# Asking for the routed tiles' rows and weights at the end of attention, turning their rows one output earlier, and collecting the last list one tile later

## The chip, the core and the metric

The kernel runs on one core of a Trainium2 chip. The metric is device microseconds of one execution, lower is better; the time quoted for a kernel is the median of its runs. A profile is one further execution, with a record of every instruction on each engine: TensorE (PE, with its weight loads as PEld), VectorE (DVE), ScalarE (ACT), GpSimd (POOL) and SyncE (SP).

## What is computed

Two layers act on `x` (4 batches, 512 tokens, 256 features, float32). Each has a gated cross-attention with 16 heads and a gated feed-forward part. The last feed-forward part is a routed one: each token goes to the one of four experts with the largest logit. Cut to what matters here:

```python
x = x + tanh(g_xattn[0]) * L0_xattn(layernorm(x), ctx)      # biases, time decay, output projection
x = x + tanh(g_ffn[0])   * L0_ffn(layernorm(x))             # ternary weights, relu
x = x + tanh(g_xattn[1]) * L1_xattn(layernorm(x), ctx)      # relu on q, k, v
# L1_ffn on h = layernorm(x), tokens t, experts e:
expert_idx = argmax(h @ W_router, -1)
a = gelu(einsum('th,ehi->tei', h, W1) + b1)                 # only the chosen expert's row is kept
y = a[t, expert_idx[t]] @ Wo + bo + h
x = x + tanh(g_ffn[1]) * (layernorm(y) * gamma + beta)
```

## The kernel before

**Attention.** The attention of both layers is a loop over 128 units `u`, four to a group of four heads; there are 32 groups. `scores(u, vs)` issues the score products (line 494): four for the maxima of a later unit (`pm`, drained on DVE by line 508) and four for the weights of this unit (`psc`, drained on ACT by the exponential in line 523). The maxima run six units ahead, so units 122 to 127 have weights alone. `slot(u)` then fills the unit with other work. Every fourth unit it does `weighted` (line 551, the product with the values) and two units later `shifted` and `divided` (lines 565, 602). What else goes in is chosen by a planner: chains of steps, each with a cost in TensorE microseconds, a `gap` (how many units must lie between it and the step before it) and a due unit. A step is taken when its chain is ready and the unit's cost stays about under `SLOT = 3.1`, or when it is due. A step that costs 0 is taken at once.

**The routed part.** The 2048 tokens are sorted by expert into 19 tiles of 128. `route(b)` normalises batch `b` (`stats`, `more_stats`, `norm`), stores the rows to the scratch `rows_d`, turns them, computes logits (`products`, line 738, `logits`, line 748) and ranks (line 764). `dispatch(i)` builds three lists of tiles: list 0 from two batches gives tiles 0 to 4, list 1 from three batches gives tiles 5 to 8, and list 2, complete, gives tiles 9 to 18. Its steps are small VectorE operations (`lists`, `token_places`, `by_tile`, `picked` in line 899, `by_expert`), then two steps that need TensorE: `collected` (line 912) and `tokens` (line 921), which end in the row numbers `get`. For a tile `j`, `fetch_rows(j)` (line 950) and `fetch_weights(j)` (line 962) are indirect DMAs issued by POOL, of 262 KB and 1.05 MB. `turn_tile(j)` (line 974) transposes the tile's rows on PE and copies them to `xs`. `hidden_half(j, f2)` (line 996) does half of the hidden products, 16 products per half, and the Gelu (line 1009). `output_tile(j)` (line 1178) does the 16 output products, `norm_tile` the layer norm on DVE with one POOL power (line 1193), and `put_tile` stores a tile by an indirect DMA on POOL (line 1205).

**What sets the order.** Within an engine instructions run in the order written; PE, DVE, ACT and POOL are scheduled by hand. Tiles 0 to 3 have their hidden products within attention (chain `ahead`, ready at `u0 + 3` of the second-layer batch 2), with the Gelu left for later. Then comes the part behind attention: the last hidden half of tile 3, the last `weighted`, `turn_tile(4)`, the last `divided`, a change of buffer pools from `att` to `moe`, the routing of the last batch (`stats3`, `more3`, `norm3`, with its layer norm on DVE and the reciprocal root on POOL, lines 330 to 340), and a queue of hidden (`"h"`) and output (`"o"`) items. In the kernel before, an `"h"` item ends with the transpose of the next tile. `steps` hangs the routing's and the last list's pieces behind items of that queue. A buffer ring limits the fetches: five row buffers (`xr`) and, for weights, two plus three.

The order of the queue before is: h4 (with the turn of 5), o0, o1, turn3, o2, products3, o3, logits3, h5 (with the turn of 6), ranks3 and the first list steps, o4, the picks, h6 (with the turn of 7), collected, o5, tokens, fetch 9, h7 (with the turn of 8), o6, h8, o7, then tile 9 and so on.

Of the kernel before, what the change touches and what calls it, by code (L numbers as in the profile page):

```python
# [20 lines left out]
B, S, D = 4, 512, 256  # L21
# [14 lines left out]
T_ALL = TT + NE - 1  # L36
# [12 lines left out]
def flamingo_kernel(ctx: ExitStack, tc: tile.TileContext, t: dict, out: bass.AP):  # L49
    nc = tc.nc  # L50
# [654 lines left out]
    def route(b, eng=None):  # L705

        st = {}

        def stats():
            st["xn"] = act.tile([P, NT, D], F32, tag="xn", name=f"xn_f1_{b}")  # L710
            first, st["more"], st["rows"] = layernorm(
                x[b], st["xn"], 1e-5, f"f1_{b}", eng
            )
            first()

        def more_stats():
            st["more"]()

        def norm():
            st["rows"]()  # L720
            (eng or nc.gpsimd).tensor_tensor(
                x[b], x[b], bet1.unsqueeze(1).to_broadcast([P, NT, D]), ALU.add
            )
            rd = rows_d[b * S : (b + 1) * S, :].rearrange("(n p) d -> p n d", p=P)
            nc.sync.dma_start(out=rd[:, :, 0:D], in_=st["xn"])
            nc.sync.dma_start(out=rd[:, :, D : 2 * D], in_=x[b])

        def turn():
            st["xT"] = act.tile([P, NC, S], F32, tag="blocks", name=f"xTf1_{b}", bufs=1)
            transposed(st["xn"], st["xT"], f"f1_{b}")  # L730

        def products():


            plT = bank_psum(f"plT{b}")[:, 0:P]
            for c in range(NC):
                for n in range(NT):
                    nc.tensor.matmul(
                        plT[n * HP : (n + 1) * HP, :], lhsT=wr[:, c, :], rhs=st["xT"][:, c, ts(n, P)],
                        start=(c == 0), stop=(c == NC - 1),  # L740
                    )
            st["lT"] = const.tile([P, P], F32, tag="dec", name=f"lT{b}")
            nc.scalar.copy(st["lT"], plT)

        def logits():

            plg = bank_psum(f"plg{b}")[:, 0:P]
            nc.tensor.transpose(plg, st["lT"], ident)
            plg = plg.rearrange("p (n e) -> p n e", e=HP)[:, :, 0:NE]
            top = sml.tile([P, NT], F32, tag="top", name=f"top{b}")  # L750
            nc.vector.tensor_reduce(top, plg, AX.X, ALU.max)
            oh = onehot[:, ts(b, NT), :]
            nc.vector.tensor_tensor(oh, plg, top.unsqueeze(2).to_broadcast([P, NT, NE]), ALU.is_ge)
            nc.vector.tensor_tensor(oh, oh, order, ALU.mult)
            nc.vector.tensor_reduce(top, oh, AX.X, ALU.max)
            nc.vector.tensor_tensor(oh, oh, top.unsqueeze(2).to_broadcast([P, NT, NE]), ALU.is_equal)

        def ranks():
            prk = bank_psum(f"prk{b}")[:, 0 : 2 * NT * NE].rearrange(
                "p (i n e) -> p i n e", i=2, e=NE  # L760
            )
            oh = onehot[:, ts(b, NT), :]
            for i, m in enumerate((before, ones)):
                nc.tensor.matmul(prk[:, i], lhsT=m, rhs=oh, start=True, stop=True)
            for n in range(NT):
                k = b * NT + n
                nc.vector.tensor_tensor(count[:, k + 1, :], count[:, k, :], prk[:, 1, n, :], ALU.add)
            nc.vector.tensor_tensor(
                rank[:, ts(b, NT), :], prk[:, 0], count[:, b * NT : (b + 1) * NT, :], ALU.add
            )  # L770

        return [
            (stats, 0, 0), (more_stats, 0, 1), (norm, 0, 1), (turn, 0.9, 1), (products, 0.6, 1),
            (logits, 0.2, 1), (ranks, 0.5, 1),
        ]
# [167 lines left out]
    def fetch_rows(j):  # L943

        have = max(n for n, first in LISTS if first <= j or n == LISTS[0][0]) * S
        if j in (3, *range(LISTS[1][1], T_ALL)) and made["behind"]:
            xg[j] = act.tile([P, 2 * D], F32, tag="xr", name=f"xr{j}", bufs=5)
        else:
            xg[j] = wts.tile([P, 2 * D], F32, tag="xg", name=f"xg{j}", bufs=4)
        nc.gpsimd.indirect_dma_start(  # L950
            out=xg[j], out_offset=None, in_=rows_d[0:have, :],
            in_offset=bass.IndirectOffsetOnAxis(ap=get[:, j : j + 1], axis=0),
            bounds_check=have - 1, oob_is_err=False,
        )

    def fetch_weights(j):

        if j < T_AHEAD or (j - T_AHEAD) % 5 < 2:
            wg[j] = weight_place(f"wg{j}")
        else:  # L960
            wg[j] = act.tile([P, NC * FF + NF], F32, tag="wg", name=f"wg{j}", bufs=3)
        nc.gpsimd.indirect_dma_start(
            out=wg[j], out_offset=None, in_=t["w1e"],
            in_offset=bass.IndirectOffsetOnAxis(ap=wrow[:, j : j + 1], axis=0),
            bounds_check=NE * P - 1, oob_is_err=False,
        )
# [51 lines left out]
    n_units = len(groups) * NT  # L1018
# [15 lines left out]
    for b in range(B):  # L1034
        first, rest = ffn0(b)
# [26 lines left out]
    def step(f, *args, cost=0, gap=0):  # L1062
        return (lambda: f(*args), cost, gap)

    def tile_steps(j):
        return [
            step(turn_tile, j, cost=0.3), step(hidden_half, j, 0, cost=1.75, gap=int(j == 0)),
            step(hidden_half, j, 1, cost=1.75),
        ]

    for b in range(B - 1):
        u0 = first_unit(1, b + 1)
        if b == 0:
            chain(route(b), u0 + 4, u0 + 13)
        elif b == 1:
            turn_0, *rest_0 = tile_steps(0)
            ahead = chain(
                [
                    *route(b), *dispatch(0), step(fetch_rows, 0), step(fetch_weights, 0),
                    step(fetch_rows, 1), step(fetch_weights, 1), step(fetch_rows, 2),  # L1080
                    step(fetch_rows, 3), (turn_0[0], turn_0[1], 2), *rest_0, step(fetch_rows, 4),
                    step(fetch_weights, 2, gap=1), *tile_steps(1), step(fetch_rows, 0),
                    step(fetch_weights, 3, gap=1), *tile_steps(2), step(fetch_rows, 1),
                    step(fetch_weights, 4, gap=1), *tile_steps(3)[:2],
                ],
                u0 + 3, n_units - 1,
            )
        else:
            routed = chain(route(b), u0 + 2, u0 + 9)
            chain(dispatch(1), n_units - LEAD, n_units - 1, routed)  # L1090
# [124 lines left out]
    for f2 in range(2):  # L1215
# [4 lines left out]
    att.__exit__(None, None, None)  # L1220
    act = ctx.enter_context(tc.tile_pool(name="moe", bufs=2))
    made["behind"] = True
    stats3, more3, norm3, turn3, products3, logits3, ranks3 = (job for job, *_ in route(B - 1, nc.vector))
    lists, token_places, by_tile, *sels, by_expert, collected, tokens = (job for job, *_ in dispatch(2))
    stats3()
    more3()
    norm3()


    steps = {  # L1230
        ("o", 1): [turn3], ("o", 2): [products3], ("o", 3): [logits3],
        ("h", 5): [ranks3, lists, token_places, by_tile], ("o", 4): [*sels, by_expert],
        ("h", 6): [collected], ("o", 5): [tokens],
    }
    first = LISTS[-1][1]
    queue = [("h", 4), *(("o", j) for j in range(4)), ("h", 5)]
    for j in range(4, T_ALL - 2):
        queue += [("o", j), ("h", j + 2)]
    queue.remove(("o", first - 1))
    queue.insert(queue.index(("h", first)), ("o", first - 1))  # L1240
    queue += [("o", T_ALL - 2), ("o", T_ALL - 1)]
    for j in (5, 3, 6, 7):
        fetch_rows(j)
        if j > 3:
            fetch_weights(j)
    for kind, j in queue:
        if kind == "h":
            for f2 in range(2):
                hidden_half(j, f2)
            if j + 1 < T_ALL and j + 1 != first:  # L1250
                turn_tile(j + 1)
        else:
            if j + 1 == first:
                turn_tile(first)
            if j < 3:
                for f2 in range(2):
                    activated(j + 1, f2)
            output_tile(j)
            norm_tile(j)
            if j > 0:  # L1260
                put_tile(j - 1)
        for job in steps.pop((kind, j), ()):
            job()
        fetch = {("o", 4): [8], ("o", 5): [9], ("o", 6): [10], ("o", 7): [11], ("o", 8): [12]}.get((kind, j))
        if fetch is None and kind == "o" and first <= j < T_ALL - 4:
            fetch = [j + 4]
        for i in fetch or ():
            fetch_rows(i)
            fetch_weights(i)
    put_tile(T_ALL - 1)  # L1270
    assert not steps

# [74 lines left out]
```

## Time and profile before

| what | value |
|---|---|
| median of 3 runs | 870.73 us (870.62 to 871.59) |
| the profiled execution's own time | 872.11 us |
| its span, first to last instruction | 870.4 us |
| mean granted TensorE clock | 0.987 of full |
| PE busy | 825.7 us (95%) |
| DVE, ACT, POOL busy | 563.8, 422.4, 278.9 us |
| bytes moved by DMA | 43.07 MB |

The page's first part gives busy time by engine, its second part cuts the span in 40 slices of 21.8 us (a digit 9 is 90% or more busy). The timeline lists instructions in order of time, equal neighbours merged, with the idle time before them in square brackets and what ended it. The table by windows gives busy time per engine in chosen stretches, the clock that was granted, and the DMA engines' share and rate. All times are from the start of the span. Attention ends and the routed tiles begin at about 716 us; the last 142 us of PE work are the tiles.

### The profile page before, as it was taken

Reading aid. Unit: us, or ns where it says so; the run is one execution under the profiler, and the core shown is the slowest. Engines: PE = TensorE matmul, PEld = TensorE weight load, DVE = VectorE, ACT = ScalarE, POOL = GpSimd, SP = SyncE. Lnnn points to the kernel's source line nnn. Section 1 sums busy time; section 2 is a strip of 40 time slices with the busy share of each in tenths; the row PEclk is TensorE's granted clock in tenths of the full one; section 3 lists DMA queues with packets and bytes.
Section 4 is the critical chain, followed back from the end, with each engine's and each line's share of the span. In section 5 each row is a group of like instructions: output and inputs, shape, how many; then the busy total and the mean of one; then the engine's idle time right before and its main releaser. Section 6 shows DMA issues by size and latency. Waiting matters only on the chain. (4 is left out here: it accounts for less than half of the span.)

```text
span 870.4 us, 13598 instructions
## 1 busy us (share of the span) xinstructions
PE 825.7 (95%) x5241; PEld 464.3 (53%) x5241; DVE 563.8 (65%) x1218; ACT 422.4 (49%) x886; POOL 278.9 (32%) x446
## 2 busy tenths in 40 slices
PE   6999999999999999999999999989999996899994
PEld 3444454435463347445555445644445545798993
DVE  6778778766856784778546864586875544843443
ACT  2475565554545452646355563366545564223331
POOL 5536365424332432401110210021033215344542
PEclk9999999999999999999999999999999998999998
DMA  9100000000000000000000010001043216055540
GB/s 319 52 1 1 1 2 2 1 1 0 2 13 25 1 1 1 26 1 1 1 1 25 1 49 1 1 1 50 1 146 110 74 62 242 26 194 173 199 162 14
DMA packets 18096, 43.07 MB, mean 49 GB/s; under 512 B 2222, under 2 KB 12208, under 8 KB 15600
## 3 DMA queue, kind: packets, MB, share of 16 engines
q0 software_dynamic: 5488, 28.13, 9.3%
q1 hardware_dynamic: 12128, 13.54, 4.6%
q8 instruction: 41, 0.67, 0.3%
q10 hardware_dynamic: 416, 0.54, 0.2%
q14 instruction: 23, 0.19, 0.1%
HBM read 35.91 MB, written 6.68 MB: 49 GB/s over the span
## 5 line engine op out<-in xcount | busy, mean ns | idle before, releaser
L508 DVE TENSOR_REDUCE m<-pm 128x1 f32<-128x512 f32 x512 | 317.1, 682 | 115.6 <-PE psc L494 112.1
L523 ACT ACTIVATE p<-psc 128x512 f32<-128x512 f32 x512 | 266.8, 603 | 154.5 <-PE psc L494 152.3
L494 PE MATMUL psc<-q,k 32*128 32x512 f32 x1024 | 280.4, 624 | 0.2 <-DVE h L672 0.2
L494 PE MATMUL pm<-k,q 32*128 32x512 f32 x1024 | 263.1, 617 | 1.3 <-ACT q L481 0.9
L526 POOL TENSOR_TENSOR p<-p,dec 128x256 f32<-128x256 f32 x128 | 93.6, 735 | 178.8 <-ACT p L523 178.8
L494 PEld LDWEIGHTS pm<-k,q 32*128 32x128 f32 x1024 | 93.1, 185 | 84.1 <-issue 50.1
L494 PEld LDWEIGHTS psc<-q,k 32*128 32x128 f32 x1024 | 106.9, 184 | 53.8 <-issue 27.3
L551 PE MATMUL po<-p,v 128*32 128x512 f32 x1024 | 116.5, 595 | 2.9 <-DVE m L508 2.9
L996 PE MATMUL pg<-xs,wg 128*128 128x128 f32 x608 | 74.1, 280 | 4.8 <-ACT xs L977 4.1
L996 PEld LDWEIGHTS pg<-xs,wg 128*128 128x128 f32 x608 | 72.1, 195 | 8.2 <-ACT xs L977 4.8
L551 PEld LDWEIGHTS po<-p,v 128*32 128x32 f32 x1024 | 31.7, 109 | 82.9 <-issue 60.5
L619 POOL TENSOR_TENSOR x<-x,o 128x256 f32<-128x256 f32 x14 | 10.2, 728 | 189.7 <-DVE o L612 128.3
L1178 PE MATMUL pyf<-wo,ha 128*128 128x256 f32 x304 | 70.6, 388 | 0.0
L1009 ACT ACTIVATE ha<-pg,wg 128x128 f32<-128x128 f32 x120 | 34.2, 368 | 71.3 <-PE pg L996 69.4
L1178 PEld LDWEIGHTS pyf<-wo,ha 128*128 128x128 f32 x304 | 57.9, 195 | 7.9 <-issue 0.4
L664 PE MATMUL ph<-xTf,w1q 128*128 128x512 f32 x128 | 60.0, 605 | 0.0
L379 PE MATMUL py_f<-w2q,h 128*128 128x256 f32 x256 | 57.2, 381 | 0.0
L557 ACT COPY oT<-po 128x512 f32<-128x512 f32 x32 | 18.7, 585 | 78.7 <-PE po L551 78.7
L379 PEld LDWEIGHTS py_f<-w2q,h 128*128 128x128 f32 x256 | 48.0, 190 | 9.4 <-DVE m L508 3.0
L1182 DVE TENSOR_TENSOR y<-y,pyf 128x256 f32<-128x256 f32 x19 | 8.0, 421 | 55.5 <-PE pyf L1178 54.9
L451 PE MATMUL pk<-cT,wk 128*128 128x512 f32 x68 | 35.4, 645 | 7.6 <-DMA cT<-in_ctxT_dram 7.3
L664 PEld LDWEIGHTS ph<-xTf,w1q 128*128 128x128 f32 x128 | 22.6, 189 | 30.4 <-issue 18.2
(223 smaller groups left out, 814.2 us busy)
## 6 DMA issues: line engine op xcount, KB each, us to landing
x<-in_x_dram SPq DMA_DIRECT2D x4, 512.0 KB, 6.7
rows_d<-xn_f SPq DMA_DIRECT2D x4, 512.0 KB, 3.0
rows_d<-x SPq DMA_DIRECT2D x4, 512.0 KB, 3.0
cT<-in_ctxT_dram SPq DMA_DIRECT2D x3, 512.0 KB, 9.1
w1q<-in_w_dram SPq DMA_DIRECT2D x1, 1024.0 KB
w2q<-in_w_dram SPq DMA_DIRECT2D x1, 1024.0 KB, 11.1
wo<-in_wo_dram SPq DMA_DIRECT2D x2, 512.0 KB
rows<-in_rows_dram SPq DMA_DIRECT2D x1, 640.0 KB, 9.0
```

Of the source, the lines that this page charges most:

```text
L379: nc.tensor.matmul(py[:, n, :], lhsT=operand(c, n0 + n), rhs=w[:, c, :], start=(c == 0), stop=(c == chunks - 1),)
L451: nc.tensor.matmul(pp, lhsT=attn_w[layer][w][:, c, ts(tt, P)], rhs=src[:, c, :], start=(c == 0), stop=(c == NC - 1),)
L494: nc.tensor.matmul(out_, lhsT=lhs[r, ts(n, P)], rhs=rhs[r, :], start=True, stop=True)
L508: nc.vector.tensor_reduce(m[:, n, 2 * pair + i, r : r + 1], pm[i], AX.X, ALU.max)
L523: nc.scalar.activation(p[:, i, :], psc[i], AF.Exp, scale=SCALE)
L526: nc.gpsimd.tensor_tensor(d, d, dec.unsqueeze(1).to_broadcast([P, 2, P]), ALU.mult)
L551: nc.tensor.matmul(po[i * HP : (i + 1) * HP, :], lhsT=v_sb[b % 2][0][:, kt, c0 : c0 + HP], rhs=ps_exp[NT * s + kt, i // 2][:, i % 2, :], s ...
L557: nc.scalar.copy(pos[s], po)
L664: nc.tensor.matmul(ph, lhsT=w1q[:, c, ts(f, P)], rhs=st["xT"][:, c, :], start=(c == 0), stop=(c == NC - 1),)
L996: nc.tensor.matmul(ph[:, f, :], lhsT=w[:, c, ts(f2 * NF // 2 + f, P)], rhs=xs[j][:, c, :], start=(c == 0), stop=(c == NC - 1),)
L1009: nc.scalar.activation(ha[:, f, :], (ha if src is None else src)[:, f, :], AF.Gelu, bias=biases[j][:, fa : fa + 1],)
L1178: nc.tensor.matmul(py, lhsT=hs[j, f // 4][:, f % 4, :], rhs=wo1[f // 4][:, f % 4, :], start=(f == 0), stop=(f == NF - 1),)
```

## The change

Four things change.

1. In the planner, each `tile_steps` has a gap of one unit between a tile's transpose and its first hidden half (before, only tile 0), and chain `ahead` becomes ready one unit later (`u0 + 4`).
2. The row and weight fetches of tiles 5, 3, 6, 7 and 8 are issued at the end of attention. Those of tiles 5 and 3 stand ahead of the last batch's `stats3`, `more3` and `norm3`, those of 6, 7 and 8 directly behind. Before, `stats3` to `norm3` stood ahead of all of them, and tile 8 was fetched behind o4.
3. A tile's transpose is an item `"t"` of the queue, placed ahead of the output that precedes its hidden products (before, behind the hidden products in front of that output).
4. `collected` moves from behind h6 to behind o5, and `tokens` from behind o5 to behind h7; the fetches of tiles 9 and 10 come behind o6 and that of 11 behind o7 (before: 9, 10 and 11 behind o5, o6 and o7). From tile 12 on the fetches stay where they were.

The order of the queue after is: h4, o0, o1, turn3, o2, products3, turn of 5, o3, logits3, h5, ranks3 and the first list steps, turn of 6, o4, the picks, h6, turn of 7, o5, collected, h7, tokens, turn of 8, o6, fetch 9 and 10, h8, o7, fetch 11, turn of 9, o8, h9, turn of 10, h10 and so on.

```diff
     def tile_steps(j):
         return [
-            step(turn_tile, j, cost=0.3), step(hidden_half, j, 0, cost=1.75, gap=int(j == 0)),
+            step(turn_tile, j, cost=0.3), step(hidden_half, j, 0, cost=1.75, gap=1),
             step(hidden_half, j, 1, cost=1.75),
         ]
...
-                u0 + 3, n_units - 1,
+                u0 + 4, n_units - 1,
...
-    stats3, more3, norm3, turn3, products3, logits3, ranks3 = (job for job, *_ in route(B - 1, nc.vector))
+    for j in (5, 3, 6, 7, 8):
+        fetch_rows(j)
+        if j > 3:
+            fetch_weights(j)
+        if j == 3:
+            stats3, more3, norm3, turn3, products3, logits3, ranks3 = (
+                job for job, *_ in route(B - 1, nc.vector)
+            )
+            stats3()
+            more3()
+            norm3()
     lists, token_places, by_tile, *sels, by_expert, collected, tokens = (job for job, *_ in dispatch(2))
-    stats3()
-    more3()
-    norm3()
...
         ("h", 5): [ranks3, lists, token_places, by_tile], ("o", 4): [*sels, by_expert],
-        ("h", 6): [collected], ("o", 5): [tokens],
+        ("o", 5): [collected], ("h", 7): [tokens],
     }
     first = LISTS[-1][1]
-    queue = [("h", 4), *(("o", j) for j in range(4)), ("h", 5)]
+    queue = [("h", 4), ("o", 0), ("o", 1), ("o", 2), ("t", 5), ("o", 3), ("h", 5)]
     for j in range(4, T_ALL - 2):
-        queue += [("o", j), ("h", j + 2)]
-    queue.remove(("o", first - 1))
-    queue.insert(queue.index(("h", first)), ("o", first - 1))
+        queue += [("t", j + 2), ("o", j), ("h", j + 2)]
+    for item, place in ((("o", first - 1), ("h", first)), (("t", first), ("o", first - 1))):
+        queue.remove(item)
+        queue.insert(queue.index(place), item)
     queue += [("o", T_ALL - 2), ("o", T_ALL - 1)]
-    for j in (5, 3, 6, 7):
-        fetch_rows(j)
-        if j > 3:
-            fetch_weights(j)
     for kind, j in queue:
         if kind == "h":
             for f2 in range(2):
                 hidden_half(j, f2)
-            if j + 1 < T_ALL and j + 1 != first:
-                turn_tile(j + 1)
+        elif kind == "t":
+            turn_tile(j)
         else:
-            if j + 1 == first:
-                turn_tile(first)
...
-        fetch = {("o", 4): [8], ("o", 5): [9], ("o", 6): [10], ("o", 7): [11], ("o", 8): [12]}.get((kind, j))
-        if fetch is None and kind == "o" and first <= j < T_ALL - 4:
-            fetch = [j + 4]
-        for i in fetch or ():
+        for i in {("o", 6): (9, 10), ("o", 7): (11,)}.get((kind, j), ()):
             fetch_rows(i)
             fetch_weights(i)
+        if kind == "o" and first <= j + 1 < T_ALL - 3:
+            fetch_rows(j + 4)
+            fetch_weights(j + 4)
```

In the built program the planner's move puts the hidden halves of tiles 1, 2 and 3 in units 118, 119, 122, 123 and 126 (before: 117, 118, 119, 121 and 122), and the statistics, the second statistics and the rows of batch 1's routing in units 100, 101 and 102 (before: 99, 100 and 101). The first fetch behind attention, that of tile 5's rows, waits for the last `divided`'s addition on DVE (line 619), whose operand shares its place.

## The prediction, made before the change was run

> **What bounds the kernel now.** I read the page's first two parts, then what PE waited for, then PE's timeline from 540 us to the end, then POOL, DVE and ACT over the same stretch. PE is busy 95% of the span, so a microsecond is won only where PE idles or runs at half clock. The page's slices dip in two places, at 65% and 83% of the span:
>
> ```profile
> PE   6999999999999999999999999989999996899994
> ...
> PEclk9999999999999999999999999999999998999998
> ```
>
> PE's timeline gives the idle time in brackets. In order: the first hidden half of tile 1, a second half, first halves of tiles 2 and 3, two units of weights, tile 5's transpose, the two outputs behind it, the last list's collection, and two outputs at the end of the kernel, for the price when nothing is in the way.
>
> ```profile
> 667.13 3.68 PE L996 MATMUL pg<-xs,wg 128*128 128x128 f32 x16 [1.70 <-ACT xs L977]
> ...
> 674.40 2.05 PE L996 MATMUL pg<-xs,wg 128*128 128x128 f32 x16
> ...
> 680.01 2.05 PE L996 MATMUL pg<-xs,wg 128*128 128x128 f32 x16 [0.69 <-ACT p L523]
> ...
> 695.52 2.05 PE L996 MATMUL pg<-xs,wg 128*128 128x128 f32 x16 [1.16 <-ACT xs L977]
> 697.50 2.99 PE L494 MATMUL psc<-q,k 32*128 32x512 f32 x16
> ...
> 727.74 0.66 PE L974 MATMUL ptx<-ident,xr 128*128 128x128 f32 x2 [7.66 <-issue]
> 728.19 8.97 PE L1178 MATMUL pyf<-wo,ha 128*128 128x256 f32 x32
> ...
> 760.12 0.94 PE L912 MATMUL pidT_d<-sel_d,tid_d 128*32 128x128 f32 x16 [2.11 <-DVE sel_d L899]
> ...
> 850.67 7.07 PE L1178 MATMUL pyf<-wo,ha 128*128 128x256 f32 x32
> ```
>
> Two of these groups are slow themselves: 3.68 us where 2.05 is usual, 8.97 where 7.07 is. The table by windows shows why: the clock is 0.50 from 726 to 732 us, and from 668 to 670.
>
> ```profile
> 726.00:727.00 1.00, 0.00 (x0) 0.00 (x0) 0.00 (x0) 0.00 (x0) 0.69 (x2) 0.50 0.65 222
> ...
> 731.00:732.00 1.00, 1.00 (x3) 0.76 (x3) 0.00 (x0) 1.00 (x5) 0.69 (x2) 0.50 1.13 441
> ```
>
> (Columns: stretch, length, busy time of PE, PEld, DVE, ACT, POOL, then clock, DMA share, GB/s.) The wait of 7.66 us is for a POOL that works late:
>
> ```profile
> 720.42 0.24 POOL L330 TENSOR_SCALAR var_f<-mv_f 128x4 f32<-128x4 f32 x1 [9.80 <-DVE mv_f L326]
> ...
> 722.72 0.20 POOL L340 TENSOR_TENSOR rstd_f<-rstd_f,fix_f 128x4 f32<-128x4 f32 x1
> 723.58 1.16 POOL L950 DMA_INDIRECT xr<-rows_d,get  x1 [0.66 <-issue]
> ...
> 731.98 1.00 POOL L962 DMA_INDIRECT wg<-in_w1e_dram,wrow  x1 [0.30 <-issue]
> ```
>
> Tile 5's rows are asked for at 723.58 and turned at 727.74, 4.16 us later.
>
> **What the Trainium skill says.** *TensorE: Matmul & The Clock Gate*, Part 1: after an idle window of about 3.4 us the clock is halved, and about 3.4 us of work brings it back. The trace agrees (0.50 behind 7.66 us of idleness, for some 4 us of work). *Perfetto Trace Analysis*, DMA Instruction — SWDGE (GPSIMD): POOL's own DSPs write the descriptors, and the profile's end is the end of that, not of the transfer. The trace agrees: an issue holds POOL for 1.0 to 1.4 us plus 0.3 to the next, and data comes later. *DMA: Bandwidth & Descriptors*, Anatomy of one DMA: about 2.0 us plus bytes over 436 GB/s, which gives an estimate of 2.6 us for 262 KB of rows and 4.4 for 1.05 MB of weights; the trace has 4.16 from the start of the issue for rows.
>
> **Part 1, the planner (units 97 to 127).** Nothing is removed or added in work. (a) Batch 1's statistics leave unit 99. Two pairs of them (577.02 to 578.16, 1.14 us on DVE) stand ahead of unit 100's maxima, for which the `po` at 578.79 waits 1.57 us on PE. Gain 1.14, plus a wait of 0.29 at 589.96 for an exponential that the rows' ACT work (2.09 us) had pushed back. That work now meets unit 103, where PE has a 1.8 us query product beside it, so I charge nothing; if that cover fails it costs up to 1. Sum **1.4**. (b) From unit 117 (661.70) to h4 (716.35) PE needs 54.65 us. Listed one by one at their full-speed prices the work is 47.7: five full units at 1.93, six of weights alone at 1.08, six halves at 1.98, three `po` at 3.57, four tile transposes at 0.4, and 7.4 for the rest (batch 2's turn and products, four maxima turns and divisions, logits, ranks, list). The other 6.95 is 1.70 + 1.70 (half clock) + 0.24 + 0.69 + 1.16, all at a half that follows its transpose or a crowded unit, and 1.46 in units 123 to 127, where two units of weights lie together and ACT (four exponentials, 2.06 us, a unit) is the slower. With the gap, each transpose's copy lies behind a unit's products, and halves fall in units 118, 119, 122, 123 and 126, so PE has 2 us of its own in three of the six ACT-bound units. ACT's load there is 12.4 us of exponentials and about 3 of copies; walked unit by unit it ends its last exponential just ahead of the last `po`, with about 0.9 us of waits left (0.3 in unit 118, where eight banks turn over, 0.34 at the last division). Gain 6.95 − 0.95 = **6.0**; bounds 4 (ACT late by one unit) and 6.6. The list's sums for tiles 5 to 8 on DVE end 2 us before PE now asks for them.
>
> **Part 2, fetches first, and o0 ahead of turn 5.** PE is freed at once: o0 and o1 go directly behind h4 (720.1 to 727.2, Gelus of tile 1 beside them), turn3, o2 to 731.8. But POOL and DVE work in order. Walked in the clock of before: tile 5's rows wait for DVE's line 619 (717.99), so issues run 718.26 to 719.42, 719.72 to 721.15, 721.45 to 722.45. Behind these stands the root of the layer norm: 722.5 to 725.0 (2.5 us, as before), 2.05 later than now. The rows of norm3 (2.6 us on DVE) end at 727.6; turn3 at 727.2 needs only the first 1.4 us, so it is not late. Then POOL has six issues, 725.6 to 733.1 (0.66, then 1.3 each), where it had four behind tile 3's. Queued behind them is the power of tile 0's norm (line 1193), on which DVE sits; behind that on DVE are tile 1's norm and the copy of turn3's second half (line 372), for which products3 waits on PE. From the power's start to that copy's end is 6.19 us now (735.12 to 741.31), so it ends at 733.15 + 6.19 = 739.3. PE has nothing from 732.1 to 739.4: **7.3 us idle**, and the clock falls again (1.7 to 2.1 us lost). Products3, turn 5 and o3 (0.3 + 0.2 + 3.55 + 0.1) put h5 at 745.3 to 745.7, against 745.66 now. So this stall isn't removed, it moves. Gain **0.2**, bounds −1 and +3.
>
> **Part 3, collected behind o5.** Now h6 ends near 758.0 and o5 starts at 762.19; of these 4.2 us only 0.7 is work. After: h5 to 749.0, ranks3 at 749.6 (it still waits for DVE), turn 6, o4, h6, turn 7, o5 to 761.2. DVE's picks, 759.3 to 761.8 now, come 0.2 earlier; 0.4 is waited. o6 starts at 766.0 instead of 769.65, that is 3.4 besides the 0.2 above. Charged against it: rows of tile 9 are asked for behind o6's norm and a put. From an o6 end to such an issue is 3.7 us (773.27 to 776.97), so 769.6 + 3.7 = 773.3, landed 3.6 to 4.2 later, 776.9 to 777.5. PE reaches turn 9 at 776.5: 0.4 to 1.0 waited, I take 0.7. Gain **2.7**. Weights of tile 9, asked for at 774.6, took 5.3 us to the end of the DMA activity in a like case (771.37), so 779.9; h9 is due at 780.9. Tile 10's are 2.8 us later and due 5 later. Turn 10 stays next to h10, with its 1.27 us wait. Later fetches keep their place; the end is unchanged.
>
> Sum: 1.4 + 6.0 + 0.2 + 2.7 = 10.3 us. Of the profiled execution's 872.11 (span 870.4 and 1.7 around it) that leaves 861.8; the median of the runs is 1.38 below that execution, so **860.4**.
>
> **Rivals.** *Part 2's stall really goes* (POOL gets through early, or the wait is not for the copy): another 7 to 9 us, about **852.5**. For it: the 7.66 us wait named in the profile is removed as such. Against it: POOL's order above. Chance 0.06. *Tile 9 late*: rows and two tiles' weights queue together, 2.6 MB at the 390 GB/s of 774 to 776 is 6.7 us; turn 9 or h9 waits 3 more: **863.5**, chance 0.13. *The planner's gain is half*: ACT or the banks fill the gaps, 3.5 of the 7.4 lost: **864**, chance 0.17. *Slower*: an issue on POOL takes as long as its data. Tiles 5 to 8 are 5.5 MB; an issue of weights that had to find room among descriptors not yet drained would take some 3 us, not 1.0. Place: the six issues ahead of tile 0's power. The forecast's 10.3 us is gone when the six take 10.3 more, 3.0 each instead of 1.3; at 3.4 it is **873**. Against it: the four issues 728 to 733, under 390 GB/s, took 1.00 each. Chance 0.03. *It does not do what it says*: PE's waits merely change places everywhere, 870; 0.02.
>
> **How the numbers follow.** The forecast, with a chance of 0.59, is 860.4, and its bounds 858 to 863. 0.2% (1.7 us) is about what this kernel's measurement can tell from no change. Range 857.5 to 865: it leaves out the early rival and the last two, 0.11, and tails of the rest. Faster 0.94, same 0.03, slower 0.03.
>
> **What would show it.** No wait of 1.7 us at a tile's first half and no half clock near 668; h4 starts 7.4 us earlier; o0 directly behind h4; then a PE wait of about 7 us at the second half of products3 (line 738) with the clock at 0.50 behind it; POOL's first line 1193 directly behind six issues; no 2 us wait at line 912; a wait under 1 us at turn 9. It is wrong if products3 isn't held, if `psc` in units 122 to 127 waits for ACT, or if h9 waits for weights.

## The result, and the profile after

| | before | after |
|---|---|---|
| median | 870.67 us (4 runs) | 861.35 us (4 runs, 860.30 to 863.67) |
| ratio | | 0.9894, 95% interval 0.9873 to 0.9916 |
| the profiled execution's own time | 872.11 us | 861.21 us |
| its span | 870.4 us | 859.5 us |
| mean granted TensorE clock | 0.987 | 0.989 |
| PE busy | 825.7 us | 821.1 us |

The forecast was 860.4 us with a range of 857.5 to 865. On a second chip the same two kernels stood at 0.9905 (0.9886 to 0.9924). To see where the 10.9 us between the two profiled spans came from, I took the starts of the same instructions in PE's two timelines and subtracted:

| stretch of PE | before | after | won | predicted |
|---|---|---|---|---|
| start to the product with the values in unit 96 | 561.49 | 559.75 | 1.74 | 0 |
| from there to that product in unit 104 (part 1a) | 38.42 | 36.82 | 1.60 | 1.4 |
| to the scores of unit 117 | 61.79 | 60.85 | 0.94 | 0 |
| to h4 (part 1b) | 54.65 | 49.52 | 5.13 | 6.0 |
| to h5 (part 2) | 29.31 | 30.17 | −0.86 | 0.2 |
| to o6 (part 3) | 23.99 | 20.92 | 3.07 | 3.4 |
| to o9 (part 3, the later fetches) | 23.28 | 23.98 | −0.70 | −0.7 |
| to the end | 77.47 | 77.49 | −0.02 | 0 |

So the total met the forecast, but not term by term: two stretches for which nothing was forecast won 2.68 us, and the terms of the change fell 2.1 short of their sum. The page's slices show the same picture: the dip at 65% is gone, the one at 83% of the span stands in the same slice as before, and the half clock, one slice before, now takes two.

```profile
PE   6999999999999999999999999999999996999994
...
PEclk9999999999999999999999999999999998899998
```

PE's timeline after, at the places shown of before: the product with the values in unit 100 (1.57 us of wait before), the first hidden half of tile 1 (1.70 before), its second half, h4, the first two outputs, products3's second half and o3 behind it, the collection (2.11 before), and the first hidden products of tile 9.

```profile
576.01 3.64 PE L551 MATMUL po<-p,v 128*32 128x512 f32 x32 [0.52 <-DVE m L508]
...
665.50 2.05 PE L996 MATMUL pg<-xs,wg 128*128 128x128 f32 x16
...
669.99 2.05 PE L996 MATMUL pg<-xs,wg 128*128 128x128 f32 x16 [0.24 <-DVE m L508]
...
706.94 3.74 PE L996 MATMUL pg<-xs,wg 128*128 128x128 f32 x32
710.51 7.07 PE L1178 MATMUL pyf<-wo,ha 128*128 128x256 f32 x32
...
730.56 0.66 PE L738 MATMUL plT<-xTf,wr 128*32 128x128 f32 x8 [8.29 <-DVE xTf L372]
731.14 0.69 PE L974 MATMUL ptx<-ident,xr 128*128 128x128 f32 x2
731.62 5.54 PE L1178 MATMUL pyf<-wo,ha 128*128 128x256 f32 x16
...
753.01 1.08 PE L912 MATMUL pidT_d<-sel_d,tid_d 128*32 128x128 f32 x32
...
772.82 3.81 PE L996 MATMUL pg<-xs,wg 128*128 128x128 f32 x32 [0.18 <-DMA wg<-in_w1e_dram,wrow]
```

Three of the four waits are gone or small. The fourth, 7.66 us at tile 5's transpose, is gone there too (the transpose at 731.14 has no bracket), but 8.29 us now stand one instruction ahead of it, at products3, and o3 takes 5.54 where 3.62 is the price when warm. The table by windows gives the reason for the latter:

```profile
726.00:730.00 4.00, 0.00 (x0) 0.00 (x0) 3.24 (x12) 0.00 (x0) 1.78 (x2) 0.50 1.01 424
730.00:735.00 5.00, 4.44 (x18) 3.38 (x19) 3.77 (x12) 0.64 (x2) 1.76 (x2) 0.50 0.36 147
```

The clock stays at 0.50 through at least the first 4.4 us of work behind the wait. POOL's timeline shows who was late: six issues in a row, and the power of tile 0's norm directly behind the last.

```profile
716.19 1.29 POOL L950 DMA_INDIRECT xr<-rows_d,get  x1 [0.51 <-issue]
717.79 1.44 POOL L962 DMA_INDIRECT wg<-in_w1e_dram,wrow  x1 [0.30 <-issue]
...
723.44 1.00 POOL L962 DMA_INDIRECT wg<-in_w1e_dram,wrow  x1 [0.30 <-issue]
724.47 0.59 POOL L1193 TENSOR_TENSOR rstd_y<-var_y,power 128x1 f32<-128x1 f32 x1
```

DVE sat 4.61 us for that power, and the copy that PE waited for came behind the rest of tile 0's norm and the whole of tile 1's:

```profile
725.09 0.22 DVE L1195 SCALAR_TENSOR_TENSOR fix_y<-rstd_y,var_y 128x1 f32<-128x1 f32 x1 [4.61 <-POOL rstd_y L1193]
...
729.82 0.68 DVE L372 COPY xTf<-pt_f 128x512 f32<-128x512 f32 x1
```

### The profile page after: what moved, and what is told of

The parts are those of the page before. It is cut to its first block, busy times and chain, and to the rows that moved or that the text cites. A ratio compares the mean times of both kernels' runs of the same rounds, so it can differ in the third digit from the quotient of the medians.

```text
span 859.5 us, 13597 instructions
## 1 busy us (share of the span) xinstructions
PE 821.1 (96%) x5241; PEld 462.1 (54%) x5241; DVE 561.7 (65%) x1218; ACT 422.5 (49%) x886; POOL 277.4 (32%) x446
```

## The experiments

Theory: the three parts act independently, part 2 wins nothing because POOL's issues hold DVE through one small power, and the stretches won without a change are chance. Rivals: the parts need each other (part 2 pays once the others are in); the copy is late for another reason; a part's gain belongs to another edit. Each kernel was timed beside the kernel before on the same chip.

### One part at a time

**The gap alone (part 1b), the gap kernel.**

```diff
-            step(turn_tile, j, cost=0.3), step(hidden_half, j, 0, cost=1.75, gap=int(j == 0)),
+            step(turn_tile, j, cost=0.3), step(hidden_half, j, 0, cost=1.75, gap=1),
```

> The kernel before with one edit: a gap of one unit between each tile's transpose and its first hidden half (part 1b alone). Theory from the trace after: units 117 to h4 shrink from 54.65 to about 49.5 us, so the time falls by 5.1 to about 865.5, and h4 starts near 711.2. My prediction's own size for this step: 6.0, so 864.7. Rival (ACT and the banks fill the gaps): 3.5 or less, 867.2. In the profile: no wait of 1.70 us at a tile's first half, no half clock near 668, the stall of 7.66 us at tile 5's transpose untouched.

Measured: 865.13 us beside 869.11, ratio 0.9955 (0.9942 to 0.9968), 4.0 us won. From unit 117 to h4 its profile has 49.53 us, as the whole change has. Tile 1's first half has no wait, and products take their usual 2.05 us:

```profile
667.84 2.05 PE L996 MATMUL pg<-xs,wg 128*128 128x128 f32 x16
```

That stretch won 5.1 us, more than the median, whose interval (2.8 to 5.0 us) leaves 5.1 out. The next kernel shows a reason.

**The ready unit alone (part 1a), the ready-unit kernel.**

```diff
-                u0 + 3, n_units - 1,
+                u0 + 4, n_units - 1,
```

> The kernel before with one edit: the routing of batch 1 becomes ready a unit later (part 1a alone). Theory: the product with the values in unit 100 waits 0.52 instead of 1.57 us, the wait of 0.29 at the key product behind it goes, and 0.27 more between them: 1.6 us less, 869.1. The further 0.85 us that the trace after won in unit 114, where the plan is the same, would be chance; the rival is that it belongs to this edit, and then it is 2.5 us, 868.2, and unit 114 takes 3.1 us again instead of 4.1.

Measured: 866.75 us beside 869.11, ratio 0.9970 (0.9959 to 0.9981), 2.4 us won. The interval, 1.7 to 3.6 us, has 1.6 just below its edge, and the median is nearer to the rival's 2.5. In the profile the stretch from unit 96 to unit 104 is 36.81 us, as after. The stretch from there to unit 117 takes 60.14 us, 1.65 less than in the profile of before, as the rival has it; but it takes 60.14 or 60.15 in the three kernels without this edit too, so it isn't the edit's. What makes the median 0.8 more than 1.6 stays open. Two lines of the profile, the product in unit 100 and the first hidden half of tile 1, which this kernel leaves where it was before:

```profile
577.44 3.64 PE L551 MATMUL po<-p,v 128*32 128x512 f32 x32 [0.52 <-DVE m L508]
...
663.57 2.05 PE L996 MATMUL pg<-xs,wg 128*128 128x128 f32 x16 [1.70 <-ACT xs L977]
```

The second line is new information. The wait of 1.70 us is the one of before, but the products behind it take 2.05 us, not 3.68: in this execution the clock was not halved. Of the four profiles that have this wait, before and the front kernel below show half clock, this one and the list kernel below don't. From unit 117 to h4 they need 54.65 and 54.60 us against 53.03 and 53.01. So about 1.6 us of part 1b's 5.1 is won only against an execution that had halved its clock; against the others it is 3.5.

**The fetches and the queue alone (part 2), the front kernel:** the changed kernel with both planner edits undone and the steps of the last list as before:

```diff
-        ("o", 5): [collected], ("h", 7): [tokens],
+        ("h", 6): [collected], ("o", 5): [tokens],
...
-        for i in {("o", 6): (9, 10), ("o", 7): (11,)}.get((kind, j), ()):
+        for i in {("o", 5): (9,), ("o", 6): (10,), ("o", 7): (11,)}.get((kind, j), ()):
```

> Part 2 alone: the kernel before with the fetches of tiles 5, 3, 6, 7, 8 at the end of attention and the transposes as items of the queue, with the planner and the last list as before. Theory (the stall moves behind POOL's six issues): no gain, 0.9 us lost, 871.5; the wait of 7.66 us at tile 5's transpose is gone and one of about 8.3 us stands at the second half of products3, with half clock behind it. Rival (the stall was removed, and the later parts of the change put it back): 7 us or more won, 863.

Measured: 870.80 us beside 869.11, ratio 1.0018 (1.0011 to 1.0026): 1.7 us slower, on the side of the theory. From h4 to h5 the profile has 30.76 us. The wait needs no help from the other parts:

```profile
736.52 0.65 PE L738 MATMUL plT<-xTf,wr 128*32 128x128 f32 x8 [8.31 <-DVE xTf L372]
737.11 0.69 PE L974 MATMUL ptx<-ident,xr 128*128 128x128 f32 x2
737.59 6.10 PE L1178 MATMUL pyf<-wo,ha 128*128 128x256 f32 x16
```

**The last list alone (part 3), the list kernel:** the kernel before with

```diff
-        ("h", 6): [collected], ("o", 5): [tokens],
+        ("o", 5): [collected], ("h", 7): [tokens],
...
-        fetch = {("o", 4): [8], ("o", 5): [9], ("o", 6): [10], ("o", 7): [11], ("o", 8): [12]}.get((kind, j))
+        fetch = {("o", 4): [8], ("o", 6): [9, 10], ("o", 7): [11], ("o", 8): [12]}.get((kind, j))
```

> Part 3 alone: the kernel before with collected behind o5, tokens behind h7, tiles 9 and 10 fetched behind o6 and 11 behind o7. Theory: the wait of 2.11 us at the collection and the bank wait beside it go, 3.1 us won between h5 and o6, 0.7 given back at turn 9 and h9: 2.4 won, 868.3. Rival (the later fetch of tile 9 costs what the list wins): a wait of 3 us or more at turn 9 or h9, 870.7.

Measured: 866.34 us beside 869.11, ratio 0.9967 (0.9957 to 0.9976), 2.8 us won. From h5 to o6 20.74 us (23.99 before), from o6 to o9 24.40 (23.28 before). Part of what is given back is tile 9's weights:

```profile
776.43 3.81 PE L996 MATMUL pg<-xs,wg 128*128 128x128 f32 x32 [0.55 <-DMA wg<-in_w1e_dram,wrow]
```

The four medians sum to −4.0 − 2.4 + 1.7 − 2.8 = −7.5 us; the medians of the whole change on two chips are 9.3 and 8.7 us below before's. The intervals of the four, each about 1 us to either side, are too wide to tell these from −7.5: no dependence between the parts is seen, one of 1 to 2 us isn't excluded, and part 2 alone pays nothing.

### What holds products3

**The changed kernel again**, as the measure for its variants:

> The changed kernel once more, beside its variants on one chip. The four runs of it so far stand at 0.9894 of the kernel before, so about 860 where the kernel before takes 869. A second profile of the same program also shows which waits and half clocks are the program's and which one execution's: the wait of 8.3 us at products3 and the half clock behind it must be there again, and the durations of unit 114 and of the stretch 28 to 32 us may differ.

Measured: 861.83 us beside 870.56, ratio 0.9905. The profile has the same wait (8.31 us, for the same copy) and half clock behind it. It differs from the first profile where theory calls it chance: between 29.5 and 32 us the clock was 0.50, and it reaches unit 96 at 561.37 instead of 559.75. The stretch from unit 104 to 117 is 60.78 us in this profile, 60.85 in the first.

**Fetches of tiles 6 to 8 behind the first norms, the spread kernel:**

```diff
-    for j in (5, 3, 6, 7, 8):
+    for j in (5, 3):
...
-        for i in {("o", 6): (9, 10), ("o", 7): (11,)}.get((kind, j), ()):
+        for i in {("o", 0): (6,), ("o", 1): (7,), ("o", 2): (8,), ("o", 6): (9, 10), ("o", 7): (11,)}.get((kind, j), ()):
```

> The changed kernel with the fetches of tiles 6, 7 and 8 behind o0, o1 and o2 instead of ahead of o0 (the power of tile 0's norm is then first on POOL). Theory (POOL's six issues hold the power, the power holds DVE, DVE holds the copy for products3): the power starts near 720.0 instead of 724.5, the copy ends near 726.2 instead of 730.5, and products3 waits 3.9 us instead of 8.3: 4.4 won, 855.5, a little more if the clock isn't halved. Rival (the copy waits for something else, DVE's own work or the rows): no gain, 860. Second rival: weights of tile 6 come late, h6 waits, 857 to 859.

Measured: 857.47 us, 4.4 less than the changed kernel beside it; ratio to before 0.9858 (0.9835 to 0.9881). PE's wait and POOL's order:

```profile
727.90 0.66 PE L738 MATMUL plT<-xTf,wr 128*32 128x128 f32 x8 [4.13 <-DVE xTf L372]
```

```profile
721.66 0.72 POOL L1193 TENSOR_TENSOR rstd_y<-var_y,power 128x1 f32<-128x1 f32 x1 [4.49 <-DVE var_y L1192]
722.56 1.17 POOL L950 DMA_INDIRECT xr<-rows_d,get  x1 [0.18 <-issue]
```

The power now waits for DVE instead of DVE for the power (h4 starts at 708.43 here, 706.94 after, so 721.66 stands for 720.17 there), and the 4.13 us that are left are DVE's two norms and their powers. No hidden product waited for weights of tile 6, 7 or 8.

**A smaller dose:** only tile 8's two fetches go back behind o4.

```diff
-    for j in (5, 3, 6, 7, 8):
+    for j in (5, 3, 6, 7):
...
-        for i in {("o", 6): (9, 10), ("o", 7): (11,)}.get((kind, j), ()):
+        for i in {("o", 4): (8,), ("o", 6): (9, 10), ("o", 7): (11,)}.get((kind, j), ()):
```

> The changed kernel with only the two fetches of tile 8 put back behind o4, as before the change: two issues fewer ahead of the first power, a smaller dose of the same cure. Theory: 2 x 1.3 us less wait at products3 (5.7 instead of 8.3), 2.6 won, 857.3, the clock still halved. Rival (it isn't the number of issues): the wait stays at 8.3 and the time at 860.

Measured: 859.56 us, 2.3 less than the changed kernel. Two issues fewer are 2.62 us less wait:

```profile
727.81 0.66 PE L738 MATMUL plT<-xTf,wr 128*32 128x128 f32 x8 [5.67 <-DVE xTf L372]
```

**The copy on ACT:**

```diff
-            transposed(st["xn"], st["xT"], f"f1_{b}")
+            transposed(st["xn"], st["xT"], f"f1_{b}", alone=b == B - 1)
```

> The changed kernel with the second half of turn3's copy on ACT, which is idle from 721 us, instead of DVE; POOL's order is as in the changed kernel. Theory: DVE is still held by the power from 720.5 to 725.1, so the wait at products3 goes and PE waits at ranks3 (line 764) for DVE's one-hot instead, some 7 us; DVE itself gets there about 3 us earlier, since it has one copy less and no late outputs to wait for: 3 won, 857. Rival (products3 was the only place that depends on it): 8 to 10 us won, 851.

Measured: 860.14 us, 1.7 less than the changed kernel. Products3 doesn't wait at all and h5 starts at 726.33 instead of 737.11, but PE pays at the ranks, for the next thing that the held DVE makes:

```profile
738.46 0.58 PE L764 MATMUL prk<-onehot,before 128*128 128x16 f32 x2 [8.40 <-DVE onehot L756]
...
739.77 5.14 PE L1178 MATMUL pyf<-wo,ha 128*128 128x256 f32 x16
```

DVE got there 3.07 us earlier (738.46 against 741.53 after), as expected; 1.5 of it went to o4 at half clock, 5.14 against 3.62, which I had not charged. Counted from h4 to h6, this profile is 1.0 us faster than the first of the changed kernel and 0.1 than the second, so of the 1.7 between the medians at most 1.0 is seen to be the copy's.

### A faster version

**All three remedies:** the spread fetches, the copy on ACT, and

```diff
-        ("o", 1): [turn3], ("o", 2): [products3], ("o", 3): [logits3],
+        ("o", 1): [turn3], ("o", 2): [products3], ("t", 5): [logits3],
```

> The changed kernel with three edits together: fetches of tiles 6, 7, 8 behind o0, o1, o2; the second half of turn3's copy on ACT; logits3 ahead of o3 instead of behind it, so that DVE makes the one-hot before tile 3's norm. Theory: products3 doesn't wait, ranks3 waits under 1 us, so PE saves the 4.1 us that the spread kernel still waited, the 0.9 us of half clock behind it and about 0.5 more at ranks3; DVE then is late for the last list's picks, 1 to 2 us waited at line 912. 857.5 - 5.5 + 1.5 = 853.5. Rival (the wait moves on whole to the next thing that DVE makes, the picks): 857. In the profile: no half clock from 720 to 740.

Measured: 855.88 us beside 870.61, ratio 0.9837 (0.9823 to 0.9850). Products3 has no wait, the ranks 1.28 us, and there is no half clock from 720 to 740. The miss of 2.4 us is at the picks: 2.12 us of wait and two of 0.18, somewhat more than the 1 to 2 expected, and the clock halved behind them and the hidden products that follow took 5.47 us instead of 3.84.

**Tile 10 turned between the halves of h9:**

```diff
             for f2 in range(2):
                 hidden_half(j, f2)
+                if j == first and f2 == 0:
+                    turn_tile(j + 1)
```

(and `("t", first + 1)` taken out of the queue)

> The kernel of the line above with the transpose of tile 10 between the two halves of h9 instead of directly ahead of h10. Theory: the 1.27 us wait of h10 for its transpose's copy goes, 1.2 won, 852.3. Rival: tile 10's rows aren't there that early, the transpose waits for them instead, and nothing is won.

Measured: 854.58 us beside 870.61, 1.3 less than the kernel above; ratio 0.9827 (0.9814 to 0.9841). In the profile h10's wait for its copy is 0.40 us, where the kernel above has 1.58. What is left at the collection:

```profile
744.62 0.94 PE L912 MATMUL pidT_d<-sel_d,tid_d 128*32 128x128 f32 x16 [1.39 <-DVE sel_d L899]
...
746.69 5.44 PE L996 MATMUL pg<-xs,wg 128*128 128x128 f32 x32
```

**Collected behind h7:**

```diff
-        ("o", 5): [collected], ("h", 7): [tokens],
+        ("h", 7): [collected], ("o", 6): [tokens],
```

> The kernel of the line above (spread fetches, copy on ACT, early logits, tile 10 turned inside h9) with the collection one item later still: collected behind h7 instead of o5, tokens behind o6 instead of h7, the fetches unchanged in the queue. Theory: DVE's last pick ended at 746.2 there and PE would ask for it at 746.8, so the waits of 1.39, 0.17 and 0.18 us at line 912 and the half clock that followed go: 2 to 3 won, 852. Rival: the last list's row numbers come later than tile 9 needs them, turn 9 or h9 waits 2 us or more, and nothing is won: 854.6.

Measured: 852.49 us (851.12 to 852.83) beside 869.80, ratio 0.9793 (0.9773 to 0.9813): faster than before and after. The collection is without a wait, turn 9 waits little for its rows, and h9 0.52 us:

```profile
747.31 1.08 PE L912 MATMUL pidT_d<-sel_d,tid_d 128*32 128x128 f32 x32
...
759.80 0.44 PE L974 MATMUL ptx<-ident,xr 128*128 128x128 f32 x2 [0.45 <-DMA xr<-rows_d,get]
```

## Why the prediction was right, point by point

**Part 1a, 1.4 predicted.** Right: 1.60 in the stretch, by itself too (36.81 us in the kernel with only this edit, 38.43 in the one with only the gap). The wait in unit 100 fell by 1.05 where I had 1.14; the rest lies in units 101 to 103.

**Part 1b, 6.0 predicted, bounds 4 to 6.6.** The mechanism is right: no wait of 1.70 us at a tile's first half and no half clock near 668. The term was mis-sized in two ways. I left 0.95 us of waits in units 117 to 127; 49.52 us less 47.7 of work leaves 1.8, of which 0.24 (669.99) and 0.50 (the last division) are waits that the timeline names, and 0.8 is in unit 122, where the products for the weights take 1.94 instead of 1.14 us. And I took the half clock near 668 for part of the kernel before; it is part of some of its executions. Against an execution without it the gain is 53.0 − 49.5 = 3.5, below my lower bound, and 4.0 is what the gap alone won by median. In unit 122 a sign that I had named as one of being wrong is there in small: the profile names a wait for ACT of 0.2 us at these products, and one for DVE of 0.3.

**Part 2, 0.2 predicted, bounds −1 and 3.** The step that decided the forecast held: the stall moved to the second half of products3, for the reason given, POOL's six issues ahead of one power that holds DVE. That is now shown three times over: with all six issues out of the way the wait is 4.13, with two out of the way 5.67, and with the copy off DVE the wait is at the ranks. The size was off by 1.0: 8.29 instead of 7.3. I had priced six issues at 7.5 us from the row of four that took 1.00 each; they took 8.25 (716.19 to 724.44), since the first two took 1.29 and 1.44, and PE was there 0.4 earlier, counted from h4. The profile of before had shown it: the two issues at the same place there took 1.16 and 1.43. The part alone is 1.7 us slower than before by median, 1.45 by its h4 to h5.

**Part 3, 2.7 predicted.** Right within 0.4: 3.07 − 0.70. The 3.07 lacks 0.3 of my 3.4, because I counted 0.7 of work at the collection, which takes 1.0 (753.01 to 754.02). The 0.70 is my number, but not all for my reason. Turn 9 was late for its rows, and only by half of what I had: PE's weight load, which takes the rows in, waited 0.48 us for them, and 0.30 is lost between o7 and o8.

```profile
768.75 0.20 PEld L974 LDWEIGHTS ptx<-ident,xr 128*128 128x128 f32 x2 [0.48 <-DMA xr<-rows_d,get]
```

Another 0.34 lies between o8 and h9, 0.18 of it a wait for tile 9's weights, which I had landed 1 us ahead of need and had named as a sign of being wrong. In the list kernel that wait was 0.55.

**The sum.** 10.3 predicted, 8.24 measured for these terms in the two profiled executions, 9.3 between the medians. That the two profiled spans differ by 10.9, so near to 10.3, is luck: the change won none of the 2.68 us beside its terms. 1.74 was lost by the profiled execution of before at its start: the same code, and the clock at 0.50 in one profile and 1.00 in the other. The window from 29.5 to 32 us, of before and then of after:

```profile
29.50:32.00 2.50, 2.50 (x10) 0.99 (x13) 0.00 (x0) 0.58 (x1) 1.76 (x2) 0.50 0.00 0
```

```profile
29.50:32.00 2.50, 2.50 (x22) 1.18 (x21) 1.36 (x3) 1.86 (x4) 1.82 (x3) 1.00 0.00 0
```

The other 0.94 lies in units 113 to 116, which need 19.12 us in the profile of before, 17.48 in all four kernels with one part, and 18.11 to 18.68 in the eight that have both planner edits. The plan for these units is the same in all. So before's profile was 1.6 unlucky there, and the kernels with both edits lose 0.6 to 1.2 us there against those with one (0.7 in the first profile after); why is open, since no run was made for it. The 9.3 between the medians is no sharper: before's own median lies between 869.11 us (41 runs) and 870.73 (3 runs) in the groups of runs here. I took 1.38, by which before's median lies under its profiled execution, off the changed kernel too, as if both profiles were equally unlucky; the changed kernel's profile (861.21) is no slower than its median (861.35).

**The rivals.** That the stall really goes: wrong, and the spread kernel shows what it would have taken. Tile 9 late by 3 more: no, 0.7 in all. The planner's gain halved: near the median of the gap alone, not as its mechanism had it. Slower, an issue as long as its data: no, the last four issues took 1.00 each while the DMA engines were full (share 1.04 at 723, 412 GB/s).

## What to carry to other kernels

Moving a fetch to an earlier place helps the engine that waits for its data and delays whatever the issuing engine has queued behind it; if that is a small operation on which another engine sits, as the power of a norm here, the stall comes back under another name, and the order to look for is the power first, then the fetches. When a wait is taken off one consumer of a late engine (the copy on ACT), ask for the next thing that PE needs from the same engine, and move that too. Before a stretch of one profile is taken for the kernel's price, look whether a half clock behind a short wait is in it: it may be that execution's.

## What the runs showed of the hardware

The Trainium skill, *TensorE: Matmul & The Clock Gate*, Part 1, has the clock halved after an idle window of about 3.4 us and calls the window free-running, so that it depends on where in it the work falls. The traces agree with the length: their record of the clock has 21 stretches of half clock between the start and the end of the kernel, and all are 3.41, 6.83 or 10.24 us long (10.24 in the first profile after, from 725.25 to 735.49). Waits of 4.13 us and more within the kernel fit too; each had half clock behind it. But waits of half that length had it too, in some executions of the same instructions:

- The wait of 1.94 us at the start (near 26 us), in every one of the 13 profiles: half clock behind it in 5, none in 8, and unit 96 is reached at 561.2 to 561.5 us in the five and at 559.6 to 560.0 in the others.
- The wait of 1.70 at tile 1's first half: 2 of 4.
- The wait of 2.11 to 2.15 at the collection: no in before and in the ready-unit kernel; yes in the gap and front kernels and in the one with all three remedies. In the gap kernel o5 behind it took 5.41 us, against 3.62.

```profile
752.85 0.94 PE L912 MATMUL pidT_d<-sel_d,tid_d 128*32 128x128 f32 x16 [2.11 <-DVE sel_d L899]
...
754.93 5.41 PE L1178 MATMUL pyf<-wo,ha 128*128 128x256 f32 x16
```

Length alone doesn't decide it: the 1.39 us at the collection of the kernel with tile 10 turned inside h9, with 0.17 and 0.18 behind it, had half clock behind it, while waits of 1.57 and 1.58 in five profiles had none. What does decide isn't shown. Each such half clock costs about 1.5 to 1.8 us. It goes with much of the spread between runs of one kernel: of the 41 runs of before on one chip, the 13 with a granted clock of 0.990 took 868.41 to 868.88 us and the 11 with 0.986 or less 869.98 to 872.04. That it stands at these waits is seen in the profiles alone.

The way back differs more than the prediction had it, with its 3.4 us of work. Behind products3's wait of 8.3 us the clock came back after 4.9 us of work in the first profile of the changed kernel, 3.1 in its second and 6.1 in the front kernel.

One more number: POOL's indirect issues took 1.29 and 1.44 us for the first two behind the layer norm and 1.00 for each one after them, to within a hundredth in two kernels (after, with four more, and the one with tile 8 put back, with two). DVE worked on the layer norm's rows beside the first two, in before as well; whether that sets them apart stays open.
